# Loading the first output-projection weights of sequence 0 between the broadcasts of sequence 1

## The chip, the cores and the metric

The kernel runs on one core of one Trainium2 chip. The metric is the device time of the program in microseconds (us); lower is better. Every time below comes from the runs of the kernel before, or from one profiled execution of it. Engines are called PE (TensorE), DVE (VectorE), ACT (ScalarE), POOL (GpSimd) and SP (SyncE, here only the issuer of transfers).

## What is computed

The program is four layers in a row, each with a layer norm before and after it and a residual add: a Mamba-like state-space layer, a gated feed-forward layer with 4-bit packed weights, an attention within each token, and a mixture layer. The change lies in the first one. Cut to that:

```python
proj = hidden_states @ W_in.T                      # (2, 512, 2048)
x, gate = proj[..., :1024], proj[..., 1024:]
...                                                # causal conv of 4 taps, silu
ts, Bm, Cm = split(x @ W_x.T); dt = softplus(rms(ts) @ W_dt.T + b_dt)
def step(state, inp):
    dA = exp(dt_t[..., None] * A)                  # 16 states per channel
    state = state * dA + (dt_t * u_t)[..., None] * B_t[:, None, :]
    y = einsum('bdn,bn->bd', state, C_t)
y = ys + x * D
y = y * silu(gate)
return y @ W_out.T                                 # the output projection
```

There are two sequences of 512 tokens, 1024 channels and 16 states. All arithmetic here is in float32.

## The kernel before

**The scan.** The 1024 channels of a sequence are 8 chunks of 128 partitions (`NCH`), the 16 states are 8 groups of 2 (`NGI`). A step `s` is one group of one chunk, so there are 64 steps for sequence 0 (s = 0 to 63) and 64 for sequence 1. In each step DVE multiplies by B (`times_B`, line 1092) and scans along time (`scan`, line 1096), ACT makes the decay factors (`exps`, line 1076), POOL multiplies by C (`times_C`, line 1102, and in some steps of sequence 1 adds the two states, line 1104), and two steps later PE adds the product into a sum over the groups (`sums`, lines 1119 and 1124, with the identity as weights). `fin(k)` (line 1130, on DVE) multiplies the finished sum of chunk k into the gate `g`; it runs in the third step of the next chunk, so `fin7`, the end of sequence 0, falls into step 66. The `bx` tiles of the steps share 6 buffers.

**The broadcasts.** B and C of a sequence are rows in memory that are loaded onto all 128 partitions, 512 KB for each group (`states`, line 560). There is one buffer for each group's B and one for its C. In steps 56 to 63, the last chunk of sequence 0, each step traces the loads of sequence 1 for its own group, after the last use of these buffers.

**PE's other work.** A generator `stream()` (line 1030) hands PE its other matmuls in a fixed order: gates and projections of sequence 1, then `fc1_expert` (line 952, a product of two weight matrices that a later layer needs), then `out_tiles` (the output projection of sequence 0, line 978), then the transposed norm and the feed-forward layer of sequence 0 (`ffn0`). Each item has an estimated cost of `MM = 0.86`, each step a budget of 3.5 less what `sums` take, and the generator is asked for more as long as the budget lasts. A `yield None` means that it must wait for a later step; `until("fin7", 0)` is such a wait. A matmul of 128x128 by 128x512 in float32 is two passes on PE and so two rows of the profile.

**The output projection.** For each of 4 token tiles i there are 4 pairs j of chunks, 16 pairs in all. `wo_pair` (line 919) loads the weights of a pair, 512 KB; two matmuls follow, one for each chunk, into a bank of PSUM. Tiles 0 and 1 are then copied and normed by `out_job`, tiles 2 and 3 by `late_tile`.

**Buffers and queues.** `wo_pair`, the gate weights, `wf1T` and `wex` of `fc1_expert` and the weights of `ffn0` all take tiles of tag `w4` in the pool `wst`, which has 3 buffers in a ring (line 73). A load into a buffer waits on SP until the tile that had it three loads before has been read. All these loads, the broadcasts and the stores of `fc1_expert` (`wfe_d`) are issued by SP in one order. `pin()` (line 407) fixes the order of PE, ACT, DVE and POOL to the order in which the program traces them. SP is not in that list; its order is settled when the program is built, by when an instruction is estimated to be ready and by the order of tracing.

Of the kernel before, what the change touches and what calls it, by code (L numbers as in the profile page):

```python
# [23 lines left out]
TB = S // P  # L24
# [4 lines left out]
NCH = D_IN // P  # L29
# [27 lines left out]
def tile_sandwich(  # L57
# [370 lines left out]
    with ExitStack() as mamba:  # L428
# [150 lines left out]
        with ExitStack() as p1:  # L579
# [10 lines left out]
            for i in range(TB + 2):  # L590
# [4 lines left out]
                if 0 <= i - 1 < TB:  # L595
                    j = i - 1
# [86 lines left out]
        with ExitStack() as p2:  # L683
# [24 lines left out]
            def spawn(gen, lag=0):  # L708
                jobs.append([now[0] + lag, gen])
# [28 lines left out]
            def bank(name):  # L738
                while not bank_free():
                    yield None  # L740
                turns.append([name, None])
                return mbank(name)
# [54 lines left out]
            def until(key, lag):  # L797
                while st.get(key, 1 << 30) + lag > now[0]:
                    yield None
# [119 lines left out]
            def wo_pair(b, i, j):  # L919
                w = wst.tile([P, 2, H], F32, tag="w4", name=f"wo{b}_{i}_{j}")  # L920
                nc.sync.dma_start(out=w, in_=w_out[j])
                return w
# [17 lines left out]
            def out_job(i, ps):  # L940
                o = jrow(f"o0_{i}")
                if i >= TB - 2:
                    yield from late_tile(i, ps, o)
                    return
                nc.scalar.copy(o, ps)
                release(f"po0_{i}")
                yield 3
                yield from add_normed(0, i, o, o)
                yield 1
                yield from norm_one(0, i, "f0")  # L950
# [25 lines left out]
                    spawn(out(), 2)  # L976

            def out_tiles():
                yield from until("fin7", 0)
                todo = [(i, j) for i in range(TB) for j in range(NCH // 2)]  # L980
                ws = {}
                for n, (i, j) in enumerate(todo):
                    for m in range(n, min(n + 2, len(todo))):
                        if m not in ws:
                            ws[m] = wo_pair(0, *todo[m])
                    if j == 0:
                        ps = yield from bank(f"po0_{i}")
                    for e in range(2):
                        c = 2 * j + e
                        nc.tensor.matmul(  # L990
                            ps, g[0][c][:, ts(i, P)], ws[n][:, e, :],
                            start=(c == 0), stop=(c == NCH - 1),
                        )
                        yield MM
                    if j == NCH // 2 - 1:
                        spawn(out_job(i, ps), 2)
# [33 lines left out]
            def stream():  # L1030
                for c in range(1, NCH):
                    yield from gate(0, c)
                xT.append(xT_tile("xT1"))
                w_in(0, 1, 0)
                yield from turned("n1", xT[1])
                for c in range(NCH):
                    yield from proj_x(c)
                yield from until("words", 2)
                yield from gate(1, 0)
                yield from gate(1, 1)  # L1040
                yield from ranks1()
                yield from gate(1, 2)
                yield from gate(1, 3)
                yield from rows1()
                for c in range(NCH - 4, NCH):
                    yield from gate(1, c)
                yield from fc1_expert()
                yield from out_tiles()
                hTs["f", 0] = xT_tile("hT_f0")
                yield from turned("f0", hTs["f", 0])  # L1050
                yield from ffn0()
# [146 lines left out]
        with ExitStack() as p3:  # L1198
# [26 lines left out]
            for i, m in enumerate(IC):  # L1225
                j, e = divmod(i, 2)
                if not e:
                    w = wst.tile([P, 2, H], F32, tag="w4", name=f"wd0_{j}")
                    n = len(IC[i : i + 2])
# [287 lines left out]
```

## Time and profile before

| | |
|---|---|
| median of 3 runs | 949.45 us (946.91, 949.45, 950.11) |
| the profiled execution | 943.15 us |
| its span, first to last instruction | 941.0 us |
| mean granted clock of TensorE | 0.966 |
| busy, share of the span | PE 91%, DVE 71%, POOL 52%, ACT 46% |
| chain that ended last, by engine | PE 40%, DVE 29%, issue 12%, DMA 5%, POOL 5%, ACT 3% |
| loads of `wo` (line 921) | 20 of 512 KB: 16 for sequence 0, 4 for sequence 1 |
| first and last of the 16 | issued at 321.83 and, of all 16, within 48.7 us |
| matmul passes of the projection (line 990) | 64, from 327.5 to 380.2 us |
| first use of sequence 1's B and C | 315.46 (DVE) and 322.42 us (POOL) |

Times in the profile count from the start of the span. An engine's idle time has a releaser, the instruction of another engine or the transfer that ended it. The granted clock is the share of full speed that PE was given in a stretch. A wait of SP is one in which a transfer could not be issued yet.

### The profile page before, as it was taken

The page shows a single profiled execution, that of the slowest core. Times are in us where ns is not written, and L with a number is a line of the kernel's source. Part 1 is how long each engine was busy: PE and PEld are TensorE (multiplying, and loading weights), DVE is VectorE, ACT ScalarE, POOL GpSimd, SP SyncE. Part 2 cuts the span into 40 slices and gives each one's busy share as a digit, 9 for nine tenths or more (in the row PEclk, how much of TensorE's full clock was granted, in tenths as well). Part 3 has the DMA queues.
Part 4 walks back from the last instruction along what each step waited for, and adds up shares of the span by engine and source line. Part 5 has one row for each costly group of instructions (what it writes and reads, how often), then busy time and mean ns, then how long its engine had stood idle before and what let it go on. Part 6 is the DMA issues. An engine that isn't in the chain of part 4 may idle for free.

```text
span 941.0 us, 7171 instructions
## 1 busy us (share of the span) xinstructions
PE 860.5 (91%) x2188; PEld 385.9 (41%) x2188; DVE 669.7 (71%) x770; ACT 428.3 (46%) x654; POOL 486.1 (52%) x356
## 2 busy tenths in 40 slices
PE   6989979879999898699999989899999998999994
PEld 3434433323544343244444434344544444445441
DVE  5778999999999998999999995525600034535235
ACT  3368875665667645656666530215320014322122
POOL 7758887767887777777788884520000000011012
PEclk9989999989999999799999999999999999999998
DMA  6549100110004954101110022356223121200101
GB/s 196 207 136 373 37 35 31 38 38 23 23 25 158 300 161 157 40 1 45 45 45 24 16 68 101 128 143 201 59 64 90 59 90 45 67 12 24 55 0 45
DMA packets 43816, 80.08 MB, mean 85 GB/s; under 512 B 7774, under 2 KB 20937, under 8 KB 43778
## 3 DMA queue, kind: packets, MB, share of 16 engines
q1 hardware_dynamic: 41506, 73.64, 24.0%
q0 software_dynamic: 1984, 5.47, 1.6%
q10 hardware_dynamic: 288, 0.52, 0.2%
q8 instruction: 17, 0.28, 0.1%
q14 instruction: 21, 0.17, 0.1%
HBM read 68.37 MB, written 11.24 MB: 85 GB/s over the span
## 4 chain that ended last, share of the span: by engine, by line
PE 40%; DVE 29%; issue 12%; DMA 5%; POOL 5%; ACT 3%; SPq 1%; DVEq 0%; POOLq 0%; ACTq 0%
DVE bx L1096 11%; DVE bx L1092 8%; PE pd L1445 6%; PE py L1124 5%; PE pup L1382 5%; PE fg L373 4%; PE fu L373 4%; PE fo L1298 3%; DMA B<-scr 2%; PE po L990 2%; DVE u L485 2%; PE fo L1235 2%; PE pr L1413 1%; POOL bx L1102 1%; PE pg L749 1%
## 5 line engine op out<-in xcount | busy, mean ns | idle before, releaser
L1102 POOL TENSOR_TENSOR bx<-bx,C 128x1024 f32<-128x1024 f32 x128 | 302.2, 2362 | 105.0 <-DVE bx L1096 77.9
L1096 DVE TENSOR_TENSOR_SCAN bx<-da,bx 128x1024 f32<-128x1024 f32 x128 | 291.7, 2279 | 0.3 <-ACT da L1076 0.2
L1124 PE MATMUL py<-bx,ident 128*128 128x512 f32 x480 | 234.5, 619 | 25.4 <-POOL bx L1102 21.8
L1076 ACT ACTIVATE da<-dt,A 128x511 f32<-128x511 f32 x256 | 176.5, 691 | 141.4 <-DVE bx L1096 136.8
L1092 DVE TENSOR_TENSOR bx<-du,B 128x1024 f32<-128x1024 f32 x127 | 152.9, 1205 | 3.8 <-POOL bx L1104 1.2
L1124 PEld LDWEIGHTS py<-bx,ident 128*128 128x128 f32 x480 | 91.9, 197 | 150.2 <-issue 97.3
L387 POOL TENSOR_TENSOR sd<-ve,half 128x4 f16<-128x4 f16 x2 | 2.1, 1042 | 113.1 <-DVE ve L385 113.1
L1311 DVE TENSOR_TENSOR it<-it,fu 128x512 f32<-128x512 f32 (+1 forms) x11 | 7.6, 687 | 73.6 <-PE fu L373 73.6
L749 PE MATMUL pg<-xT,w_g 128*128 128x512 f32 x114 | 56.3, 624 | 0.7 <-ACT dt L573 0.7
L1382 PE MATMUL pup<-hT_l,wup 128*128 128x512 f32 x128 | 56.2, 593 | 0.0
L1445 PE MATMUL pd<-wdn,hid 128*128 128x512 f32 x128 | 55.3, 593 | 0.0
L129 POOL TENSOR_TENSOR rs_lo<-ve_lo,mhalf 128x1 f32<-128x1 f32 x8 | 5.4, 680 | 76.7 <-DVE ve_lo L127 76.7
L1235 PE MATMUL fo<-wd,it 128*128 128x512 f32 (+1 forms) x88 | 40.0, 616 | 3.6 <-DMA wd<-wd_d 3.6
L1021 PE MATMUL fg<-hT_f,wg 128*128 128x512 f32 (+1 forms) x88 | 42.5, 594 | 0.0
L373 PE MATMUL fg<-hT_f,wg 128*128 128x512 f32 (+1 forms) x88 | 41.9, 615 | 0.7 <-ACT hT_f L173 0.7
L485 DVE SCALAR_TENSOR_TENSOR u<-px,ch,u 128x511 f32<-128x511 f32 (+2 forms) x48 | 35.9, 747 | 8.3 <-ACT u L478 7.1
L1021 PE MATMUL fu<-hT_f,wu 128*128 128x512 f32 (+1 forms) x88 | 40.4, 594 | 1.4 <-ACT dt L573 1.4
L373 PE MATMUL fu<-hT_f,wu 128*128 128x512 f32 (+1 forms) x88 | 39.8, 593 | 0.0
L1298 PE MATMUL fo<-wd,it 128*128 128x512 f32 (+1 forms) x88 | 39.6, 592 | 0.0
L1445 PEld LDWEIGHTS pd<-wdn,hid 128*128 128x128 f32 x128 | 24.2, 190 | 30.7 <-issue 30.1
L1310 ACT ACTIVATE it<-fg 128x512 f32<-128x512 f32 (+1 forms) x11 | 6.6, 597 | 65.7 <-PE fg L373 65.7
L1382 PEld LDWEIGHTS pup<-hT_l,wup 128*128 128x128 f32 x128 | 23.9, 190 | 28.2 <-issue 28.2
(243 smaller groups left out, 1168.2 us busy)
## 6 DMA issues: line engine op xcount, KB each, us to landing
wo<-in_W_outT SPq DMA_DIRECT2D x20, 512.0 KB
B<-scr SPq DMA_DIRECT2D x16, 512.0 KB
C<-scr SPq DMA_DIRECT2D x16, 512.0 KB
wg<-wgu_d SPq DMA_DIRECT2D x10, 512.0 KB
wu<-wgu_d SPq DMA_DIRECT2D x10, 512.0 KB
w_x<-in_W_in SPq DMA_DIRECT2D x8, 512.0 KB
wgu_d<-w_gu POOLq DMA_DIRECT2D x16, 256.0 KB, 2.4
w_g<-in_W_in SPq DMA_DIRECT2D x8, 512.0 KB
```

What stands on the lines that cost most here:

```text
L373: nc.tensor.matmul(ps[:m], w[:, kc, e * P : e * P + m], hT[:, kc, :], start=(kc == 0), stop=(kc == KH - 1),)
L749: nc.tensor.matmul(ps, w[:, k, ts(e, P)], xT[b][:, k, :], start=(k == 0), stop=(k == KH - 1))
L1021: nc.tensor.matmul(ps[:m], wt[j][a][:, kc, e * P : e * P + m], hT[:, kc, :], start=(kc == 0), stop=(kc == KH - 1),)
L1076: nc.scalar.activation(das[s % 2][:, i, 1:], st["dt", b, c][:, 1:], AF.Exp, scale=A[:, c, n : n + 1])
L1092: nc.vector.tensor_mul(bx, st["du"].unsqueeze(1).to_broadcast([P, NG, S]), Bbs[b][gi])
L1096: nc.vector.tensor_tensor_scan(flat, das[s % 2].rearrange("p n t -> p (n t)"), flat, 0.0, ALU.mult, ALU.add)
L1102: nc.gpsimd.tensor_mul(bxs[s], bxs[s], Cbs[b][s % NGI])
L1124: nc.tensor.matmul(st["y"], ident, bx[:, i, :], start=False, stop=last)
L1235: nc.tensor.matmul(fo[t], its[i][:m, ts(t, P)], w[:m, e], start=(i == 0), stop=(i == len(IC) - 1),)
L1298: nc.tensor.matmul(fo[t], its[i][:m, ts(t, P)], w[:m], start=(i == 0), stop=(i == len(IC) - 1),)
L1382: nc.tensor.matmul(ps, w[:, kc, ts(e, P)], src[kc], start=(kc == 0), stop=(kc == KH - 1))
L1445: nc.tensor.matmul(pd, hid[kc][:, ts(i, P)], wdn[kc], start=(kc == 0), stop=(kc == INT // P - 1),)
```

## The change

The first two loads of the projection's weights are traced when the generator reaches `out_tiles`, ahead of the wait for `fin7`, and so five steps earlier, in step 61 in place of step 66. From then on the load of pair n+2 is traced before the matmuls of pair n, where before it was that of pair n+1.

```diff
             def out_tiles():
+                todo = [(i, j) for i in range(TB) for j in range(NCH // 2)]
+                ws = {n: wo_pair(0, *todo[n]) for n in range(2)}
                 yield from until("fin7", 0)
-                todo = [(i, j) for i in range(TB) for j in range(NCH // 2)]
-                ws = {}
                 for n, (i, j) in enumerate(todo):
-                    for m in range(n, min(n + 2, len(todo))):
-                        if m not in ws:
-                            ws[m] = wo_pair(0, *todo[m])
+
+                    if n + 2 < len(todo):
+                        ws[n + 2] = wo_pair(0, *todo[n + 2])
                     if j == 0:
                         ps = yield from bank(f"po0_{i}")
```

## The prediction

> **What bounds the kernel now.** I read the page first: DVE is busy 71% of the span and PE 91%, but the change touches one place only, so the stage decides. I looked for the loads of `wo` by tile, then for the chain of waits around them, the waits of DVE and PE there, SP's queue, and last the granted clock. The chain of waits from 321 to 360 us (start, length, what):
>
> ```profile
> 319.05 2.35 POOL bx L1102
> ...
> 321.42 0.32 SPq L560
> ...
> 321.83 5.52 DMA wo<-in_W_outT
> 327.35 0.14 issue
> 327.48 7.08 PE po L990 x12
> 334.57 0.86 PE py L1119 x2
> ...
> 340.58 4.29 PE po L990 x10
> ...
> 358.99 0.87 PE py L1124 x2
> 359.87 0.02 issue
> 359.89 0.04 DVE g L1130
> ```
>
> SP issues the last broadcast of sequence 1 at 321.42 and the first weights right behind it at 321.83; they land 5.5 us later, and PE starts the projection with them. From there to 359.87 PE is the bound: every row of the chain is PE's, and DVE waits for it at its end. The waits of DVE from 318 to 362 us (us in total, times, longest) and those of PE from 318 to 330:
>
> ```profile
> DVE g L1130 <- PE py L1124: 3.4, 1, 3.4
> DVE bx L1092 <- POOL bx L1104: 1.2, 1, 1.2
> ```
>
> ```profile
> PE py L1124 <- POOL bx L1102: 2.2, 1, 2.2
> PE po L990 <- DMA wo<-in_W_outT: 1.3, 1, 1.3
> ```
>
> DVE, which otherwise scans without a pause, stands 4.6 us in this stretch. The 1.2 us before the `bx` at 337.24 is put down to POOL, but that `bx` takes over the buffer that the late PE sums of step 64 (334.4 to 337.1) set free, so I count it as PE's too. PE's own visible wait for the weights is 1.3 us. Yet its twelve matmul passes took 7.08 us, where ten later took 4.29, 0.429 each. The stretches show why; the columns are PE, PEld, DVE, ACT and POOL busy, granted clock, DMA share, GB/s:
>
> ```profile
> 314.67:318.09 3.42, 2.62 (x7) 0.96 (x6) 3.22 (x3) 1.38 (x2) 2.37 (x1) 1.00 0.82 280
> 318.09:321.50 3.41, 1.20 (x4) 0.25 (x2) 3.41 (x3) 1.38 (x2) 2.34 (x1) 1.00 0.93 290
> 321.50:324.92 3.42, 3.42 (x4) 1.10 (x4) 3.42 (x3) 2.65 (x3) 2.35 (x1) 0.50 0.97 237
> 324.92:328.33 3.41, 2.10 (x5) 0.78 (x5) 3.41 (x4) 2.10 (x4) 2.52 (x2) 1.00 1.00 385
> 328.33:331.74 3.41, 3.41 (x5) 1.33 (x4) 3.41 (x3) 2.48 (x4) 3.30 (x2) 0.50 0.31 101
> 331.74:335.16 3.42, 3.42 (x9) 1.52 (x8) 3.42 (x3) 1.71 (x3) 2.46 (x2) 1.00 0.74 229
> ```
>
> The clock changes on a raster of 3.41 us. A stretch in which PE was busy for 1.20 or 2.10 us is followed by one at 0.50; after 2.62 us it stays at 1.00. The pause for the weights lies in 324.92 to 328.33, and the next stretch runs at half speed.
>
> **The change part by part.** *Removed and added instructions:* none. There are 16 loads of 512 KB and 64 matmul passes before and after. The order traced on PE, ACT, DVE and POOL is untouched, because `wo_pair` never yields to the planner; only SP, which `pin()` leaves out, gets another order.
>
> *The first two loads.* They are traced five steps earlier, after the last `fc1_expert` matmuls. Their place in the ring of three `w4` buffers does not change: the first takes the buffer of the last gate weights (last read at 306.1), the second that of `wf1T` (last read at 313.0), the third that of `wex` (same time). That SP can carry a load ahead of its traced place is in the rows: `wex`, traced with `fc1_expert`, was issued at 289.99, between two broadcasts. So I take 306 and 313 us for them, instead of 321.83 and 322.31. Bounds: no move at all (gain 0), or any move early enough for them to be landed at 325.9; anything in between is the same to PE.
>
> What PE then does: the last instruction before the projection is `pv`, from 325.06, two passes, so its pipeline is free at 325.06 + 2 x 0.43 = 325.92. Twelve passes at 0.429 end at 331.07, where the row of before has the next matmul (line 1119) at 334.40. The gain on PE is 3.33 us. It has two terms: 327.48 - 325.92 = 1.56 us of pause, and 334.40 - 327.48 - 5.15 = 1.77 us of half clock.
>
> The second term is where a rule of the Trainium skill speaks against the change. "TensorE: Matmul & The Clock Gate", section "Why this matters for your kernels", says that pauses up to about 3 us between bursts do no harm: a whole idle window is needed to bring the clock down. By that rule a pause of 1.3 us cannot be what halved the clock at 328.33, removing it would leave the half stretch, and the sum would be 1.56 us. The rows say otherwise: 2.10 us busy of 3.41 was enough for 0.50, and also 1.93 of 3.41 at 236.17 to 239.58. I go by the rows: 3.33 us. The same page (section "What's actually happening") says the window runs freely, so its place against the kernel differs from run to run; the trace, one execution, cannot show that. With the raster elsewhere the gain lies between 1.6 us (a half stretch, 1.7, lies over the projection in the new kernel too) and 3.4 (full clock already at 321.44: `pv` ends at 324.1 and the pause is 327.48 - 324.1); I keep 3.3, near the upper end, because it is the only raster seen.
>
> *The load of pair n+2 in place of n+1.* Nothing changes: the loads of before wait for the buffer, not for their traced place. In the waits of SP, 13 of the 16 `wo` loads wait for PE's `po`, 37.4 us in total, so they already leave the moment a pair is read; SP has no other load between 321.83 and 371.91. The third load, now traced first after `fin7`, goes where the first went, at 321.83. It must be there at 325.92 + 8 x 0.43 = 329.4; in the trace of before all three had landed by about 329.2 (DMA share 1.05 in 327 to 328, 0.16 in 329 to 330), and now only one of them leaves after 321. The fourth leaves when pair 0 is read, 327.7 instead of 330.44, and is needed at 331.07 + 6 x 0.43 = 333.7; such a load landed about 3 us after its issue (issue 330.44, DMA share back to 0.49 in 333 to 334). No new wait.
>
> *The queues passed.* On SP the two loads now stand before some broadcasts and a `wfe_d` store. Each broadcast fills B or C of sequence 1 for a use eight steps after its buffer falls free; the last B leaves at 318.11 and is used at 340.57. The engines of DMA are 0.72 to 1.02 busy from 302 to 321 us; two more transfers of 512 KB at 385 GB/s take 2.7 us. A delay of 3 to 5 us is covered by over 15 us of slack; without that cover each us would be a us of DVE. POOL's queue isn't passed.
>
> *The end.* PE reaches the sums of `fin(8)` at 359.87 - 3.33 = 356.5. DVE without its two waits would be there at 359.89 - 4.62 = 355.3. So PE is still last, the `bx` wait is gone, the `g` wait shrinks from 3.4 to 1.3 us, and DVE gains all 3.3. Behind it, from 364 to 440 us, DVE waits for nobody, and what follows hangs on it, so the gain is carried to the end. Sum for the profiled execution: span 941.0 + 2.15 around it = 943.15, less 3.3 = 939.8. It is a quick one; I take the same microseconds off the median, 949.45 - 3.3 = 946.1 (0.35%). A difference of 0.3%, 2.85 us, is about what a measurement of this kernel can tell.
>
> **The rivals.**
> - *A: pause and half clock go.* 946.1; from 944.8 (all 4.6 us of DVE's waits) to 946.6. For: the rows above. Chance 0.55.
> - *B: only the pause goes,* because the raster lies elsewhere or the rule holds, or part is lost later: 949.45 - 1.6 = 947.9. Chance 0.17.
> - *C: SP keeps the old order,* the first two loads still behind the last broadcast: 949.4. For: in before no `wo` load went ahead, though its buffer was free at 306. Against: they were traced behind the broadcasts then, and are now traced before some of them. Chance 0.14.
> - *D: slower.* SP's order is fixed when the program is built, by estimated times, and is pinned to nothing. If the earlier PE reshuffles it in the stage after the scan, the chain there, which goes through POOL's `w_d` (line 329, starts 580.53, 582.75, 584.77, 586.79: one each 2.02 us) and SP's rows 591.97 to 596.48, is stretched by 2.02 us for each word that a load of the second part stands behind. Against: nothing traced there changes. Two places (4.0) only undo the gain; from three (6.1) on it is slower: 949.45 - 3.3 + 6.1 = 952.2. Chance 0.14.
>
> **How the numbers follow.** The forecast is A, 946.1. Faster by over 0.3%: A, 0.55. Within 0.3%: B and C, 0.31. Slower: D, 0.14. Leaving out D, the range runs from A's fast edge to C, with 0.5 us at each end for the measurement: 944.3 to 949.9. It takes in gains and no change; A alone is 944.8 to 946.6.
>
> **What would show it.** Right: SP issues two `wo` loads before 315 us; no wait of `po` for a DMA; twelve `po` passes in about 5.2 us behind `pv`; DVE's waits between 318 and 362 us 1.3 us in place of 4.6. Wrong: `wo` first at 321.8 (C); the pause gone but a stretch at 0.50 still over the projection (B); a broadcast that DVE or POOL waits for; new waits on SP after 570 us (D).

## The result, and the profile after

The changed kernel takes 944.93 us (median of 22 runs, 943.33 to 950.37), the kernel before in the same sessions 949.11 (946.2 to 952.46): ratio 0.9964, 95% interval 0.995 to 0.9978, or 3.4 us (2.1 to 4.7). The ratio is that of the means, 945.61 and 949.01 us; the two medians lie 4.2 us apart. The forecast was 946.1, which was 3.3 us less than the median shown then, 949.45.

The profiled execution of the changed kernel is the slowest of its 22 (950.37 us): its span is 948.4 us, where that of before was 941.0. So the two are compared by distances inside the stage. `fin(6)`, ahead of the stage, comes at 299.59 us in place of 297.42: all of the new trace is 2.17 us late before the change can act. Below, "on the scale of before" means less these 2.17 us.

The chain of waits of the changed kernel, from 300 to 362 us:

```profile
323.58 0.32 SPq L560
...
323.95 7.74 DMA wo<-in_W_outT
331.69 0.04 issue
331.74 1.98 PE po L990 x4
333.72 0.86 PE py L1119 x2
...
358.15 0.87 PE py L1124 x2
359.02 0.02 issue
359.04 0.04 DVE g L1130
```

A load of `wo` is in the chain again, and again behind the last broadcast, but it is another one: PE waits for it with only four passes left before the sums, not twelve. SP's queue in the changed kernel shows that this is the third load:

```profile
313.17 0.39 SPq L921 DMA_DIRECT2D wo<-in_W_outT  x1
313.65 1.24 SPq L971 DMA_DIRECT2D wfe_d<-fe  x1
316.31 0.32 SPq L560 DMA_DIRECT2D C<-scr  x1
316.72 0.39 SPq L921 DMA_DIRECT2D wo<-in_W_outT  x1
...
323.58 0.32 SPq L560 DMA_DIRECT2D C<-scr  x1
323.95 0.43 SPq L921 DMA_DIRECT2D wo<-in_W_outT  x1
```

The first two left at 313.17 and 316.72, between the broadcasts. PE's rows in the changed kernel:

```profile
325.52 1.12 PE L568 MATMUL pv<-dtT,wdt 33*128 33x512 f32 x2
326.57 3.70 PE L990 MATMUL po<-wo,g 128*128 128x512 f32 x8
331.74 1.98 PE L990 MATMUL po<-wo,g 128*128 128x512 f32 x4 [1.46 <-DMA wo<-in_W_outT]
333.56 1.02 PE L1119 MATMUL py<-u,dg 128*128 128x512 f32 x2
```

The projection follows `pv` without a pause, its first eight passes run at 0.43 us each, and then comes the wait for the third pair, 1.46 us. The waits of DVE from 318 to 362 us (us in total, times, longest):

```profile
DVE g L1130 <- PE py L1124: 1.7, 1, 1.7
DVE bx L1092 <- DVE du L1090: 0.2, 1, 0.2
```

The wait of `bx` for POOL, 1.2 us, is gone (a new one of 0.2 is for DVE's own `du`), and that of `g` is half. What it comes to is read from the two `fin` rows of line 1130, first in before, then in the changed kernel:

```profile
325.42 0.66 DVE L1130 TENSOR_TENSOR g<-g,py 128x512 f32<-128x512 f32 x1
...
359.89 0.69 DVE L1130 TENSOR_TENSOR g<-g,py 128x512 f32<-128x512 f32 x1 [3.42 <-PE py L1124]
```

```profile
327.58 0.66 DVE L1130 TENSOR_TENSOR g<-g,py 128x512 f32<-128x512 f32 x1
...
359.04 0.69 DVE L1130 TENSOR_TENSOR g<-g,py 128x512 f32<-128x512 f32 x1 [1.72 <-PE py L1124]
```

`fin(7)` to `fin(8)` took 34.5 us and takes 31.5. That is the measure of the stage in what follows. Two further distances of the same rows are used: `fin(9)` to `fin(10)`, 28.7 before and 29.8 now, and the last, `fin(14)` to `fin(15)`, 27.7 and 28.1.

### The profile page after: what moved, and what is told of

It is laid out like the page before. It is cut to its first block, busy times and chain, and to the rows that moved or that the text cites. A ratio compares the mean times of both kernels' runs of the same rounds, so it can differ in the third digit from the quotient of the medians.

```text
span 948.4 us, 7168 instructions
## 1 busy us (share of the span) xinstructions
PE 862.0 (91%) x2188; PEld 386.8 (41%) x2188; DVE 670.2 (71%) x770; ACT 428.9 (45%) x654; POOL 487.1 (51%) x356
## 4 chain that ended last, share of the span: by engine, by line
PE 35%; DVE 31%; issue 14%; POOL 6%; ACT 5%; DMA 2%; SPq 1%; DVEq 0%; POOLq 0%; ACTq 0%
DVE bx L1096 12%; DVE bx L1092 9%; PE pup L1382 5%; PE py L1124 4%; PE fu L373 4%; PE fg L373 4%; PE pd L1445 4%; PE fo L1298 3%; DVE u L485 2%; POOL bx L1102 2%; PE fo L1235 2%; PE po L990 2%; PE pg L749 1%; PE pr L1413 1%; POOL w_d L329 1%
## 5 line engine op out<-in xcount | busy, mean ns | idle before, releaser
L373 PE MATMUL fu<-hT_f,wu 128*128 128x512 f32 (+1 forms) x88 | 42.4, 625 | 0.0
L1021 PE MATMUL fu<-hT_f,wu 128*128 128x512 f32 (+1 forms) x88 | 40.4, 594 | 1.4 <-ACT dt L573 1.4
L1445 PEld LDWEIGHTS pd<-wdn,hid 128*128 128x128 f32 x128 | 24.9, 194 | 31.8 <-issue 31.2
L1382 PEld LDWEIGHTS pup<-hT_l,wup 128*128 128x128 f32 x128 | 24.5, 195 | 28.8 <-issue 28.8
```

The source lines that it names most:

```text
L373: nc.tensor.matmul(ps[:m], w[:, kc, e * P : e * P + m], hT[:, kc, :], start=(kc == 0), stop=(kc == KH - 1),)
L1021: nc.tensor.matmul(ps[:m], wt[j][a][:, kc, e * P : e * P + m], hT[:, kc, :], start=(kc == 0), stop=(kc == KH - 1),)
L1382: nc.tensor.matmul(ps, w[:, kc, ts(e, P)], src[kc], start=(kc == 0), stop=(kc == KH - 1))
L1445: nc.tensor.matmul(pd, hid[kc][:, ts(i, P)], wdn[kc], start=(kc == 0), stop=(kc == INT // P - 1),)
```

## The experiments

Ratios are to the kernel before on the same chip, with 95% intervals. "Stage" is `fin(7)` to `fin(8)` in the profile of that run.

| run | what | ratio | stage, us | fin(9) to fin(10) | fin(14) to fin(15) |
|---|---|---|---|---|---|
| (before) | first profile | 1 | 34.5 | 28.7 | 27.7 |
| e10_before_again | before, second profile | | 34.4 | 30.0 | 28.2 |
| e11_before_third | before, third profile | | 36.1 | 29.0 | 27.8 |
| e2_later_only | only the look-ahead | 0.9994 (0.998 to 1.0007) | 34.5 | 28.7 | 27.7 |
| (the change) | first profile | 0.9964 (0.995 to 0.9978) | 31.5 | 29.8 | 28.1 |
| e9_change_again | the change, second profile | 0.9966 (0.9945 to 0.9986) | 31.1 | 30.1 | 28.2 |
| e4_warm_pause | before, pause filled | 0.9978 (0.9964 to 0.9992) | 32.7 | 28.8 | 27.7 |
| e12_warm_again | the same, second profile | | 33.2 | 30.2 | 28.3 |
| e3_three_early | three loads early | 0.9962 (0.9946 to 0.9979) | 29.7 | 30.3 | 29.3 |
| e5_start_early | projection ahead of `fin7` | 1.0051 (1.0035 to 1.0068) | 31.7 | 31.7 | 26.3 |
| e6_three_warm_f0 | three early, second pause filled | 0.9946 (0.9925 to 0.9967) | 29.7 | 28.5 | 27.7 |
| e7_warm_tail | the change, last pause filled | 0.9961 (0.9945 to 0.9978) | 30.1 | 28.8 | 27.5 |
| e8_three_warm_both | three early, both filled | 0.9933 (0.9907 to 0.9959) | 31.4 | 28.5 | 27.5 |

**e2_later_only: one part of the change alone.**

```diff
-                ws = {n: wo_pair(0, *todo[n]) for n in range(2)}
                 yield from until("fin7", 0)
+                ws = {n: wo_pair(0, *todo[n]) for n in range(2)}
```

> The first two loads stay behind the wait for fin7; only the second part of the change is made, the load of pair n+2 in place of n+1. My theory: the loads wait for their buffers, so nothing changes; ratio to before 1.000 within 0.1%, first wo load again right behind the last broadcast, DVE's waits in the stage near 4.6 us. Rival (the look-ahead of two pairs is what gains): ratio near 0.996, like the full change.

Measured: 0.9994, and every distance of the stage as in before. The look-ahead of two pairs is worth nothing here. The other half, the first two loads early and the later ones traced as before, is no kernel of its own: it gives the same instructions in the same order on every engine as the full change. So the gain is that of the first two loads.

**e4_warm_pause and e12_warm_again: the half clock by itself.** Nothing is loaded earlier; PE only has something to do while it waits.

```diff
                     if j == 0:
                         ps = yield from bank(f"po0_{i}")
+                    if n == 0:
+                        for _ in range(2):
+                            nc.tensor.matmul(ps, ident, g[0][0], start=True, stop=True)
```

> The kernel before with two more matmuls (four passes, 1.7 us) into the bank of the first projection tile, whose result the first real matmul overwrites; they need no wo and fill the pause of PE. Nothing is loaded earlier. Theory 1 (the pause halves the granted clock over the projection): the pause costs as much as before, but the stretch at 0.50 behind it goes, PE gains up to 1.7 us, ratio 0.9985 (0.9975 to 1.000). Theory 2 (only the pause itself counted, the clock fell for the earlier pause): ratio 1.000, the half stretch is still there.

> The kernel before with the pause filled by two matmuls, for a second profile. If the filling keeps the clock up: fin(7) to fin(8) 32.5 to 33 us, no stretch at 0.50 over the projection, wherever the raster lies. If its first profile only had a lucky raster: near 34.5 us with such a stretch.

PE's rows in e4_warm_pause:

```profile
325.76 1.98 PE L990 MATMUL po<-g,ident 128*128 128x512 f32 x4
328.76 5.42 PE L993 MATMUL po<-wo,g 128*128 128x512 f32 x12 [1.01 <-DMA wo<-in_W_outT]
334.01 1.02 PE L1122 MATMUL py<-u,dg 128*128 128x512 f32 x2
```

The projection still waits for its first load, but its twelve passes take 5.42 us in place of 7.08. Time falls by 0.22% (2.1 us; the interval is 0.8 to 3.4): the half clock was a cost of its own, and the 1.77 us of the forecast lie within the interval. In the profile the stage shrinks by 1.7 us. The second profile shows 5.42 us again, and no half clock over the projection. Its stage, 33.2 us, lies just over the 32.5 to 33 expected, because the weights landed later: PE waited 1.47 us for them behind the four passes.

**e10_before_again and e11_before_third: before, with the raster elsewhere.**

> The kernel before once more, for a profile with the clock's raster elsewhere. Theory 1 (the pause ahead of the projection halves the clock behind it at most places of the raster): fin(7) to fin(8) 34 to 35 us, with a stretch at 0.50 over the projection. Theory 2 (only at the place of the first profile): 32.5 to 33 us, no stretch at 0.50 between 325 and 335 us.

> The kernel before a third time, for one more place of the raster. The same two theories: 34 to 35 us with a stretch at 0.50 over the projection, or 32.5 to 33 us without.

PE's rows in e10_before_again, and below them the stretches of the clock on that run's raster (the columns as in the prediction):

```profile
323.31 1.12 PE L568 MATMUL pv<-dtT,wdt 33*128 33x512 f32 x2
327.43 7.00 PE L990 MATMUL po<-wo,g 128*128 128x512 f32 x12 [3.00 <-DMA wo<-in_W_outT]
334.26 1.02 PE L1119 MATMUL py<-u,dg 128*128 128x512 f32 x2
```

```profile
323.78:327.19 3.41, 0.65 (x2) 0.00 (x0) 3.41 (x4) 3.37 (x4) 2.45 (x2) 1.00 0.98 303
327.19:330.61 3.42, 3.19 (x4) 1.50 (x5) 3.42 (x3) 2.19 (x4) 3.22 (x3) 0.51 0.55 211
330.61:334.02 3.41, 3.41 (x9) 1.51 (x8) 3.41 (x3) 1.48 (x3) 2.46 (x2) 0.99 0.51 154
```

At this place the clock was full at 321.4, so `pv` came 1.75 us sooner and the pause for the weights was 3.0 us, not 1.3; the end is the same, 334.26. In e11_before_third the pause was 3.4 us and the half clock held for 6.8 us: 36.1 us. That is more than the 34 to 35 expected, by the second half stretch. All four profiles of the old order of loads (e2_later_only among them) have a half stretch over the projection, so theory 1 holds; all three of the changed kernel (e7_warm_tail among them) have none.

**e3_three_early: the wait that is late next.**

```diff
-                ws = {n: wo_pair(0, *todo[n]) for n in range(2)}
+                ws = {n: wo_pair(0, *todo[n]) for n in range(3)}
...
-                    if n + 2 < len(todo):
-                        ws[n + 2] = wo_pair(0, *todo[n + 2])
...
+                    if n + 3 < len(todo):
+                        ws[n + 3] = wo_pair(0, *todo[n + 3])
```

The last two lines stand behind the two matmuls of pair n.

> Three loads ahead of the wait for fin7, all three buffers, and later loads traced behind the pair that frees their buffer. My theory: in the changed kernel the third load, issued at 324 and landed 7.7 us later, has become the last wait of PE (1.5 us); taken away, PE reaches the sums of fin(8) up to 1.7 us earlier and DVE's remaining wait of 1.7 us goes: ratio to before 0.9950 (0.994 to 0.9964), 1 to 1.5 us below the changed kernel. Rival (PE's pause is not what ends last any more, the scan is): the same as the changed kernel, 0.9964.

In its profile the twelve passes run in one piece:

```profile
325.47 1.12 PE L568 MATMUL pv<-dtT,wdt 33*128 33x512 f32 x2
326.52 5.42 PE L987 MATMUL po<-wo,g 128*128 128x512 f32 x12
331.78 1.02 PE L1118 MATMUL py<-u,dg 128*128 128x512 f32 x2
```

The stage shrinks to 29.7 us, 1.8 less than in the changed kernel, and DVE no longer waits for PE in it. But the time does not follow: 0.9962, where the changed kernel has 0.9964. In the stage my theory was right; the time, at the slow end of the theory's range and beside the rival's figure, does not decide. Its own profile tells where the 1.8 us may have gone: 0.5 us more between `fin(9)` and `fin(10)`, 1.2 us more at the last `fin`. In the first of these PE comes out of pauses in the norm behind the projection. The granted clock is the column before the last two, in the changed kernel and then in e3_three_early, from 0.3 to 0.5 us ahead of `fin(9)`:

```profile
395.00:401.00 6.00, 4.81 (x6) 2.16 (x7) 6.00 (x6) 4.55 (x7) 3.76 (x2) 0.50 0.00 0
```

```profile
393.50:399.50 6.00, 5.01 (x6) 2.19 (x7) 6.00 (x6) 4.39 (x6) 3.96 (x2) 0.53 0.00 0
```

In the first profile of before the same six us had 0.67.

**e6_three_warm_f0: that restart.** On top of e3_three_early, in `turned`, the four passes go into the bank of the next transposes:

```diff
                     tp = yield from bank(f"tp_{name}_{i}")
+                    if name == "f0" and i in (1, 2):
+                        for _ in range(2):
+                            nc.tensor.matmul(tp, ident, g[0][0], start=True, stop=True)
```

> Three loads early, and besides, two more matmuls into the bank of the second and third transposed tile of the norm behind the projection, overwritten by the transposes; they fill pauses of PE around 389 and 394 us. Theory 1 (the 1.8 us that three early loads gained at fin(8) are given back because PE restarts at half clock behind fin(9)): fin(9) to fin(10) takes 28.7 to 29.1 us in place of 30.3, ratio 0.9945 to 0.9955. Theory 2 (it is given back elsewhere): fin(9) to fin(10) stays over 29.5 us and the ratio near 0.9962.

In its profile:

```profile
393.50:399.50 6.00, 5.46 (x19) 2.55 (x17) 6.00 (x6) 4.57 (x7) 4.13 (x2) 1.00 0.00 0
```

Full clock, 28.5 us from `fin(9)` to `fin(10)`, and 0.9946, as theory 1 has it. That the filling removes the half clock at this restart is shown. That this is what keeps the gain of the third load is not: from `fin(8)` to the last `fin` this profile is 3.5 us shorter than that of e3_three_early, and only 1.8 of them lie between `fin(9)` and `fin(10)`. The other 1.7 lie at the last `fin` (27.7 in place of 29.3), where nothing was filled here. The intervals of 0.9962 and 0.9946 overlap as well.

**e7_warm_tail and e8_three_warm_both: the last sums,** with e9_change_again, the changed kernel, beside them on the same chip.

```diff
                     if part == 0:
+                        if s == NS:
+                            warm = mbank("warm")
+                            for _ in range(2):
+                                nc.tensor.matmul(warm, ident, g[1][0], start=True, stop=True)
                         if 0 <= s - 2 < NS:
```

> The changed kernel with two more matmuls into a free bank, ahead of the last two sums of the scan, in the 2.4 us in which PE waits for POOL there. If the half clock over the last eight passes (5.3 us in place of 3.4) is on the path: the last fin comes 1 to 1.8 us earlier, ratio to before 0.9945 to 0.9955. If the stage behind it hangs on something else: as the changed kernel, 0.9964.

> Three early loads and both fillings of PE's pauses. If both half stretches are on the path: ratio 0.993 to 0.9945, the fastest of all. If only one is: 0.9945 to 0.9955; if none is: 0.9962.

> The changed kernel as it is, as the measure beside the other three on the same chip: ratio 0.995 to 0.9978, and a second profile of it with another place of the clock's raster: PE's pauses ahead of the projection gone, its wait for the third load within 0 to 1.7 us, fin(7) to fin(8) 31 to 32 us in place of 34.5.

The rows of the last sums in the changed kernel, then in e7_warm_tail:

```profile
564.36 5.65 PE L1124 MATMUL py<-bx,ident 128*128 128x512 f32 x8 [2.40 <-POOL bx L1102]
```

```profile
557.49 1.88 PE L1164 MATMUL warm<-g,ident 128*128 128x512 f32 x4
560.06 1.98 PE L1124 MATMUL py<-bx,ident 128*128 128x512 f32 x4 [0.68 <-POOL bx L1102]
563.15 1.98 PE L1124 MATMUL py<-bx,ident 128*128 128x512 f32 x4 [1.11 <-POOL bx L1102]
```

The eight slow passes without a break, 5.65 us, have become two groups of four of 1.98 us. But PE now waits 1.11 us for POOL between them, so the half clock had mostly hidden a wait. The last `fin` comes 0.2 to 0.8 us sooner than in most profiles, not 1 to 1.8, and 0.9961 beside 0.9966 of e9_change_again is no difference. The first of the two theories failed, the second holds.

With both fillings and three early loads, e8_three_warm_both, 942.32 us (6 runs), ratio 0.9933, is the quickest version tried. Its interval overlaps that of e6_three_warm_f0, and how much of the lead is the last pause stays open. Its stage is 31.4 us and not 29.7, because the half clock lay ahead of the projection in this execution, over the sums of step 63:

```profile
321.52 3.68 PE L1126 MATMUL py<-bx,ident 128*128 128x512 f32 x4 [2.22 <-POOL bx L1104]
325.13 1.12 PE L568 MATMUL pv<-dtT,wdt 33*128 33x512 f32 x2
326.18 5.42 PE L990 MATMUL po<-wo,g 128*128 128x512 f32 x12
```

In the first profile of before these four passes took 3.68 us too, and `pv` started at 325.06. This is thus the one profile with early loads on the raster that the forecast was worked out on.

**e5_start_early: the projection ahead of `fin7`.** On top of the change, the wait moves to the pair that needs it:

```diff
-                yield from until("fin7", 0)
                 for n, (i, j) in enumerate(todo):
...
+                    if n == NCH // 2 - 1:
+                        yield from until("fin7", 0)
                     for e in range(2):
```

> The changed kernel, with the wait for fin7 moved from ahead of the projection to ahead of its fourth pair, the first that reads the last gate chunk: six matmuls of the first tile start in steps 61 to 65. My theory: PE has idle time there (0.8 and 2.2 us ahead of the sums of steps 62 and 63), so these matmuls cost little and the stretch from 326 to 359 us in which PE is the bound gets shorter by up to 2.6 us of passes plus the wait for the third load; DVE's remaining wait of 1.7 us goes: ratio 0.9945 to 0.996. Rival: the matmuls push the sums of steps 60 to 63 back and with them fin7, and it is the same as the changed kernel or up to 1 us slower.

It is slower than before by 0.5%. This is worse than both expectations: some 8 us slower than the changed kernel, where the rival allowed 1. Its waits of PE from 310 to 330 us, and those of DVE from 396 to 549 (the latter were 1.2 us in the changed kernel):

```profile
PE po L991 <- DMA wo<-in_W_outT: 2.5, 2, 1.9
```

```profile
DVE it L1010 <- PE fu L1022: 8.4, 5, 3.2
```

The first line is the rival: the loads cannot be there by then, PE waits for them in front of sums, and `fin7` comes 2.6 us later. The larger part I had not foreseen: the feed-forward multiply on DVE (line 1010) waits for PE 8.4 us in all, in five places, and chunks that took 29.1 to 29.3 us take 30.3 to 30.9. My reading, which no run tests, is that all later work of PE is asked for earlier here, and that this multiply is then pinned at a place where PE is not ready for it.

## Why the prediction was right, point by point

*The order of SP and the pause.* Two loads between the broadcasts, 311.0 and 314.6 us on the scale of before (313.17 and 316.72 less 2.17), beside 306 and 313 in the forecast; DVE and POOL waited for no broadcast. Right in what counts, and rival C is refuted. The first load left 5 us later than forecast: I had let it go when its buffer fell free, but in SP's order it stands behind a broadcast of C, and SP's broadcasts waited 3.9 us for POOL to free a C buffer just before it (308 to 314 us). It still landed in time.

*The half clock.* Right in size, and a term of its own: e4_warm_pause takes away nothing else and gains 2.1 us, 1.7 of them seen in the stage. A pause of 1.3 us was followed by a half stretch, and so was one of 3.0. The first speaks against the rule that pauses up to about 3 us between bursts do no harm (the Trainium skill, "TensorE: Matmul & The Clock Gate", "Why this matters for your kernels"). The second lies at the rule's edge. But the reading that I put in its place, so many us busy in a stretch, was too simple as well. In the changed kernel, on its own raster (counted back from the places where the clock changes later in that profile), these two stretches with 1.72 and 1.95 us busy are followed by full clock:

```profile
319.67:323.08 3.41, 1.72 (x4) 0.41 (x3) 3.41 (x3) 1.38 (x2) 1.87 (x1) 1.00 0.91 311
323.08:326.50 3.42, 2.89 (x6) 0.97 (x6) 3.42 (x3) 2.06 (x3) 2.39 (x2) 1.00 1.01 414
...
329.91:333.32 3.41, 1.95 (x5) 0.87 (x5) 3.41 (x3) 1.91 (x3) 3.23 (x3) 1.00 0.87 291
333.32:336.74 3.42, 3.42 (x9) 1.51 (x9) 3.42 (x3) 1.71 (x3) 2.47 (x2) 1.00 0.44 169
```

In before, 2.10 us busy had been followed by 0.50. What exactly decides stays open.

*"No new wait" for the third load.* This step failed in part. It landed at 331.69, or 329.5 on the scale of before, where I had said 329.2; but with the clock full ahead of `pv`, PE wanted it at 327.8 and not at 329.4. The waits were 1.46 us in the first profile, 1.10 in e9_change_again, about 0.3 in e7_warm_tail (twelve passes in 5.75 us). It cost nothing against the forecast, since the faster clock ahead of it had brought PE there about 1.6 us early, and PE went on when the load landed. That the two cancel is luck: the forecast took over the raster of before, on which the clock ahead of `pv` is half, and all three profiles of the changed kernel had it full there.

*DVE's waits and the stage.* Forecast 1.3 us left of 4.6, and 3.3 us gained, which would be a stage of 31.2. Measured 1.7, 1.4 and 0.3 us left of the `g` wait (the change, e9_change_again, e7_warm_tail), and a stage of 31.5, 31.1 and 30.1 us in place of 34.4 to 36.1. On the raster of the forecast, with a third load early, e8_three_warm_both has 31.4.

*"The gain is carried to the end."* Nearly. From `fin(7)` to the last `fin` the four profiles of the old order took 244.0, 244.0, 245.6 and 246.0 us, the three of the changed kernel 242.5, 242.6 and 239.5 (the last one with its pause at the end filled). In two of three profiles of the changed kernel PE's restart behind `fin(9)` lies longer at half clock, about 1.1 to 1.4 us over the 28.7 of before. A second profile of before has 30.0 there too, so the change alone does not make it; that the place of the raster does is likely, not shown. With three early loads, 29.7 us of stage brought no more time than 31.5 (e3_three_early).

*The later loads.* Nothing, as forecast: e2_later_only. *Rival D* (SP's order behind the scan): the order of SP behind the projection's first loads did not change, and its waits for `w_d` after 570 us are 21.6 us before and 21.4 now. (Of the four starts of `w_d` that I counted with, the first two are 2.22 us apart and only the others 2.02; nothing hangs on it.)

## What to carry to other kernels

A pause of an engine can cost more than its length: filling PE's wait with useless matmuls, with no data earlier, brought 2.1 us (0.8 to 3.4) here, beside 3.4 for the change. When a load is moved ahead of a stage, ask which of the next loads takes its place as the last one; and when a stage gets shorter, follow the gain to the next restart before counting it. The two earlier loads did no harm here because the broadcasts that they passed had over 15 us of slack. Earlier work in an order that a planner hands out is another matter, since everything behind it moves too: it cost some 8 us in e5_start_early.

## What I had not expected of the hardware

A load of 512 KB that was issued at 323.95, behind other broadcasts and loads, landed 7.7 us later, where one of before, issued at 330.44 into idle DMA engines, needed about 3. Around the projection the half clock came in stretches of 3.41 us, in e11_before_third in one of 6.8, but equal pauses were followed by 0.50 in one execution and by 1.00 in another: that of 2.2 us ahead of the sums of step 63 by 0.50 in the first profile of before and by 1.00 in e10_before_again. Runs of one and the same program differed by up to 12 us (942.68 to 954.63 for before, 36 runs on one chip). The distances of `fin` rows inside one profile were far steadier where the clock was full: `fin(10)` to `fin(11)` is 29.1 us in every profile but that of e5_start_early.
